# A Perceiver block on one core: half of each pair's 16 turning strips move from SyncE to ScalarE, and the self-attention's divisions run one step later

## The chip, the cores and the metric

The kernel runs on one core of one Trainium2 chip. The time is the device time of one execution in microseconds (us). Three runs of the kernel before took 1126.07, 1129.47 and 1130.55 us; the median is 1129.47 us. Engines are named as the profile names them: PE is TensorE (PEld its weight loads), DVE is VectorE, ACT is ScalarE, POOL is GpSimd, SP is SyncE, which only issues DMAs here. A "q" behind a name (ACTq, SPq) is that engine's sequencer, which issues DMAs and waits on semaphores.

## The reference

Eight batches of 128 rows and 512 columns go through three layers, each added to its input, each after a layernorm without weights:

```python
# cross-attention, 8 heads of 64; context is (8, 2048, 384)
q = (x @ Wq);  k = (context @ Wk);  v = (context @ Wv)
attn = softmax(einsum('bihd,bjhd->bhij', q, k) * 64**-0.5, axis=-1)
x = x + (einsum('bhij,bjhd->bihd', attn, v) @ Wo + bo)
# self-attention over the 128 rows, causal, one head of 512, softmax over the *query* axis
logits = where(causal, -inf, einsum('bik,bjk->bij', queries, keys))
probs = softmax(logits, axis=1) / sqrt(512)
x = x + xn + einsum('bij,bjv->biv', probs, values)     # xn: the normed x
# feed-forward, 2048 hidden units, values rounded to small float formats
x = x + float_quantize(float_quantize(relu(xn @ w1.T + b1)) @ float_quantize(w2).T + bq)
```

All inputs are float32.

## The kernel before, in words

**Steps.** The cross-attention runs as 32 steps: for each batch b (0 to 7) the eight heads are taken as four pairs m (0 to 3), loop at L881 to L950. A step (b, m) does these things:

- `scores` (L549): PE makes eight banks of 128x512 scores (tile `sc`); DVE copies each bank into the SBUF tile `p`, finding the row maxima on the way (L568), and then makes `nm`, the negated and scaled maximum of each head (L576).
- `attend` (L603): PE multiplies the previous pair's turned probabilities `pT` with the values into `po` (L611).
- a **unit**, a generator of PE work that belongs to the next batch or another stage: mostly a k projection or a v projection, written as a product of blocks in 20 small products instead of 24 (`block_product`, L371). Each product is four weight loads and matmuls on the page's rows (two matmuls, each counted with its passes), and takes about 0.86 us of PE. Seven of the results are taken out of PSUM by ACT copies (`take`, L385) and the others are added by DVE (L388, L391).
- `exps` (L579): ACT takes the exponent of each of the two heads in place in `p`, 2.0 us each.
- `turns` (L587): DVE turns `p` in eight pieces as 32x32 squares (L595), four of them after each exponent, and then 16 DMAs, here called **strips**, carry 32 partitions with 4 KB each (128 KB) from `p` to their place in `pT` (L600). Strip (g, a) goes from partitions of group a to partitions of group g; it can start when the two pieces g of the two heads are turned. In 29 of the 32 steps SP issues all 16; in the last three steps, (7, 1) to (7, 3), SP and POOL issue eight each.

There is one `p` tile (apart from one step) and one `pT` tile. So the DVE copies of the next step's scores into `p` wait until the strips have read it, and the strips wait until `attend` has read `pT`.

**Order.** PE, ACT and DVE follow an order written out by hand through the cross-attention (`manual_schedule`, L156, L262, L264): instructions stand on these engines in the order in which the program calls them. The DVE and ACT orders end at L963 and L964; SP's and POOL's orders come from the scheduler. A generator is cut into pieces by `yield`; `first_of` runs it to the next `yield`, `all_of` to its end. In `block_product` the first `yield` (L396) stands after the first of the seven ACT copies, the second (L407) after the fifth. In a usual step ACT's order is: exponent of head 0, copy 1, exponent of head 1, copies 2 to 7. Copy 6 (product 0, output (3, 1)) frees the bank `z2` for product 9, the 13th in PE's order; copy 7 frees `z1` for the 14th.

DMAs that SP and ACT issue share eight completion semaphores, handed out in turn. A DMA waits until the one that had its semaphore before has landed.

**Self-attention.** During the steps (7, 1) to (7, 3) the units are the self-attention of batches 0 to 3: `keys`, `weights_and_values`, `values_and_reads` (L717 to L803). `weights` (L754) makes for each row block r the logits `lg` (L764), their maximum (L768), the exponent `e` on ACT with its sum `den` (L771), and at once the reciprocal (L773) and the scaling (L774) on DVE. `read` (L800) multiplies `e` with the values. The other four batches and the feed-forward follow after the steps.

Of the kernel before, what the change touches and what calls it, by code (L numbers as in the profile page):

```python
# [9 lines left out]
F32 = mybir.dt.float32  # L10
# [7 lines left out]
P = 128  # L18
# [49 lines left out]
def tile_perceiver_block(  # L68
# [21 lines left out]
    nc = tc.nc  # L90
    B, S, D = x.shape
# [18 lines left out]
    SQ = 32  # L110
    Q = P // SQ
# [11 lines left out]
    def bank(name):  # L123
        return ps_one.tile([P, 512], F32, tag="bank", name=name)
# [244 lines left out]
    kts, vts, ps_, sums, qts, turned_, pos, nms, wides = [{} for _ in range(9)]  # L369
# [179 lines left out]
    def scores(b, m):  # L549

        q = qts[b][:, m, :]
        if m == 0:
            sums[b] = small.tile([P, NH], F32, tag="sums", name=f"sums_{b}")
        mx = small.tile([P, 2, NJ], F32, tag="mx", name=f"mx_{b}_{m}", bufs=3)

        home, tag = (ktp, "kt0") if (b, m) == (B - 1, 2) else (pp, "p")
        p = home.tile([P, Q, 2, J // Q], F32, tag=tag, name=f"p_{b}_{m}")
        for n in range(NJ):  # L560
            pair = [bank(f"sc_{b}_{2 * m + i}_{n}") for i in range(2)]
            for i in range(2):
                r = slice(i * DH, (i + 1) * DH)
                nc.tensor.matmul(  # L564
                    pair[i], q[r, :], kts[b, m // 2][r, m % 2, ts(n, 512)], start=True, stop=True
                )
            for i in range(2):
                nc.vector.tensor_scalar(  # L568
                    p[:, :, i].rearrange("p g (t i) -> p t g i", i=SQ)[:, ts(n, Q)],
                    pair[i].rearrange("p (t g i) -> p t g i", g=Q, i=SQ),  # L570
                    1.0, None, ALU.mult, ALU.max, accum_out=mx[:, i, n : n + 1],
                )
        top = small.tile([P, 2], F32, tag="top", name=f"top_{b}_{m}", bufs=3)
        nc.vector.reduce_max(top, mx, axis=AX.X)
        nm = small.tile([P, 2], F32, tag="nm", name=f"nm_{b}_{m}", bufs=3)
        nc.vector.tensor_scalar(nm, top, -SCALE, None, ALU.mult)  # L576
        ps_[b, m], nms[b, m] = p, nm
# [9 lines left out]
    def turns(b, m):  # L587

        p = ps_[b, m]
        pt = ptp.tile([P, Q, 2, J // Q], F32, tag="pT", name=f"pT_{b}_{m}")
        for i in range(2):
            for g in range(Q):
                nc.vector.transpose(p[:, g, i], p[:, g, i])  # L595
        for g in range(Q):
            for a in range(Q):

                eng = nc.gpsimd if b + 1 == B and m > 0 and a % 2 else nc.sync
                eng.dma_start(pt[ts(g, SQ), a], p[ts(a, SQ), g])  # L600
        turned_[b, m] = pt.rearrange("p a h (t i) -> p h t a i", i=SQ)

    def attend(b, m):  # L603


        if m == 0:
            pos[b] = ps_acc.tile([P, NK * S], F32, tag="po", name=f"po_{b}")
        for jt in range(NJT):
            v = vts[b, jt // 8].rearrange("p i t n -> p (i t) n")
            for h in range(2):  # L610
                nc.tensor.matmul(  # L611
                    pos[b][h * DH : (h + 1) * DH, ts(m, P)].rearrange("p (a i) -> p a i", a=Q),
                    v[:, jt % 8, ts(2 * m + h, DH)],
                    turned_[b, m][:, h, jt],
                    start=(jt == 0), stop=(jt == NJT - 1),
                )

    def inverse_sums(b):

        rden = small.tile([P, NH], F32, tag="rden", name=f"rden_{b}")  # L620
        nc.vector.reciprocal(rden, sums[b])
        wide = tmp.tile([P, NH, DH], F32, tag="t", name=f"wide_{b}")
        nc.vector.tensor_copy(wide, rden.unsqueeze(2).to_broadcast([P, NH, DH]))
        wides[b] = wide.rearrange("p h d -> p (h d)")
# [70 lines left out]
    rows = {}  # L695
# [21 lines left out]
    class SelfAttention:  # L717
# [36 lines left out]
        def weights(self, b):  # L754

            i = b % GB
            ps = bank(f"pl_{b}")
            for k in range(NK):
                nc.tensor.matmul(
                    ps[:, :S], self.kt[:, k, ts(i, S)], self.xt[:, k, ts(i, S)],  # L760
                    start=(k == 0), stop=(k == NK - 1),
                )
            lg = self.pool.tile([P, S], F32, tag="lg", name=f"lg_{b}", bufs=2)
            nc.vector.scalar_tensor_tensor(  # L764
                lg, ps[:, :S], c_rows[:, b : b + 1], self.mask, ALU.add, ALU.add
            )
            nm = small.tile([P, 1], F32, tag="snm", name=f"snm_{b}", bufs=4)
            nc.vector.reduce_max(nm, lg, axis=AX.X, negate=True)  # L768
            e = self.pool.tile([P, S], F32, tag="e", name=f"e_{b}", bufs=4)
            den = small.tile([P, 1], F32, tag="sden", name=f"sden_{b}", bufs=4)  # L770
            nc.scalar.activation(e, lg, AF.Exp, bias=nm, accum_out=den)  # L771
            r = small.tile([P, 1], F32, tag="sr", name=f"sr_{b}", bufs=4)
            nc.vector.reciprocal(r, den)  # L773
            nc.vector.tensor_scalar(e, e, r, RSK, ALU.mult, ALU.mult)  # L774
            self.es[b] = e
# [15 lines left out]
            yield  # L791

        def values_and_reads(self, rows):
            for r in rows:
                self.values(r)
            for r in self.rows:
                self.read(r)
            yield
# [7 lines left out]
    def all_of(unit):  # L806
        for _ in unit:
            pass

    def first_of(unit):  # L810
        next(unit)
        return unit
# [68 lines left out]
    for b in range(B):  # L881
        last = b + 1 == B
        for m in range(NK):
            scores(b, m)
            unit = None
            if m > 0:
                attend(b, m - 1)
            elif b > 0:

                attend(b - 1, NK - 1)  # L890
            if m == 0:
                unit = v_proj(b, 1)
            elif not last and m == 1:
                unit = v_proj(b + 1, 0)
            elif not last:
                unit = k_proj(b + 1, m - 2)
            elif m == 1:
                unit = sa0.keys()
            elif m == 2:
                unit = sa0.weights_and_values(sa0.rows[:2])  # L900
            else:
                unit = sa0.values_and_reads(sa0.rows[2:])
            if b == m == 0:

                keys = k_proj(0, 1, (1,))
                first_of(keys)
                first_of(keys)
                exps(b, m, 0)
                all_of(keys)
            else:  # L910
                exps(b, m, 0)
                if unit and not (last and m > 0):
                    first_of(unit)
            exps(b, m, 1)
            if b == m == 0:
                all_of(both_weights())
            if m == 0 and b > 0:
                turned = normalized_first(b - 1)
                if last:
                    bring_last_rows()  # L920
            if m == 1 and b > 0 and not last:
                row_stats(b - 1)
            if m == 2 and b > 0 and not last:
                norm_rows(b - 1)
            turns(b, m)
            if m == 0 and b > 0:
                ot = normalized(b - 1, turned)
            if m == NK - 1:
                inverse_sums(b)
            if unit:  # L930
                all_of(unit)
            if m == 1 and b > 0 and not last:
                row_scale(b - 1)
            if m == 2 and b > 0 and not last:
                nc.scalar.dma_start(xtd[:, :, ts(b - 1, S)], stats[b - 1])
                nc.scalar.dma_start(xr[:, b - 1, :], xs[b - 1])
            if m == 2 and b < B - 2:
                load_x(b)
            if m == 2 and last:
                bring_rows()  # L940
            if m == 3:
                next_half(b + 2, 0)
            if m == 0:
                next_half(b + 1, 1)
                if not last:
                    load_q(b + 1)
                if b > 0:
                    project(b - 1, ot)
                if last:
                    sap, w, sa0 = enter_self_attention()  # L950
    sa1 = SelfAttention(1, sap, w)
# [85 lines left out]
    all_of(sa1.keys())  # L1037
    for r in sa1.rows:
        sa1.weights(r)
    sa1.values(B - 1)  # L1040
    xf0 = normed_rows(0, "xt0")
    for r in sa1.rows:
# [5 lines left out]
    for i in range(1, len(pairs)):  # L1048
        last = i + 1 == len(pairs)
# [66 lines left out]
```

## Time and profile before

| What | Value |
|---|---|
| Runs | 1126.07, 1129.47, 1130.55 us, median 1129.47 |
| The profiled execution's own time | 1125.05 us |
| Its span | 1123.0 us |
| Granted TensorE clock, mean | 0.996 |
| PE busy | 1101.8 us (98% of the span) |
| DVE busy | 812.1 us (72%) |
| ACT busy | 380.8 us (34%) |
| POOL busy | 243.4 us (22%) |
| Strips issued by SP | 488, 128 KB each, median 2.4 us from issue to landing |
| Strips issued by POOL | 24, 128 KB each, median 4.7 us from issue to landing |
| Exponents, 128x2048 | 64, mean 2003 ns |
| Turning pieces on DVE, 128x512 | 256, mean 679 ns |
| ACT copies out of a unit's banks, v and k | 224, mean 589 and 562 ns |

The share of an engine is an average over the stages. DMA-issuing instructions are not counted as busy, so ACT's 34% holds no issue time. In a row of the timeline the first number is the start in us from the span's start, the second the length; the bracket at its end tells the idle time before it and what ended it. In a row of the waits the three numbers are the total in us, how often, and the longest.

### The profile page before, as it was taken

Reading aid. Unit: us, or ns where it says so; the run is one execution under the profiler, and the core shown is the slowest. Engines: PE = TensorE matmul, PEld = TensorE weight load, DVE = VectorE, ACT = ScalarE, POOL = GpSimd, SP = SyncE. Lnnn points to the kernel's source line nnn. Section 1 sums busy time; section 2 is a strip of 40 time slices with the busy share of each in tenths; the row PEclk is TensorE's granted clock in tenths of the full one; section 3 lists DMA queues with packets and bytes.
Section 4 is the critical chain, followed back from the end, with each engine's and each line's share of the span. In section 5 each row is a group of like instructions: output and inputs, shape, how many; then the busy total and the mean of one; then the engine's idle time right before and its main releaser. Section 6 shows DMA issues by size and latency. Waiting matters only on the chain.

```text
span 1123.0 us, 17002 instructions
## 1 busy us (share of the span) xinstructions
PE 1101.8 (98%) x6250; PEld 830.7 (74%) x6254; DVE 812.1 (72%) x1736; ACT 380.8 (34%) x623; POOL 243.4 (22%) x358
## 2 busy tenths in 40 slices
PE   9999999999999999999999999999999979999997
PEld 5485888878777787878787878777887535687775
DVE  5975577778767877878776778767876574976656
ACT  3323333232223232433242232223232321663332
POOL 0244220440044015203500440054001220000001
PEclk9999999999999999999999999999999999999999
DMA  9476235644454455345545644554347475300001
GB/s 328 134 181 169 80 85 120 156 130 112 106 156 115 105 141 133 85 113 150 128 96 122 157 129 114 116 154 108 95 97 223 102 185 192 113 1 20 10 10 38
DMA packets 71858, 134.83 MB, mean 120 GB/s; under 512 B 28240, under 2 KB 36448, under 8 KB 70752
## 3 DMA queue, kind: packets, MB, share of 16 engines
q1 hardware_dynamic: 61120, 113.03, 39.4%
q0 software_dynamic: 3312, 11.03, 3.2%
q10 hardware_dynamic: 7344, 9.70, 2.8%
q8 instruction: 49, 0.80, 0.3%
q14 instruction: 33, 0.27, 0.1%
HBM read 54.01 MB, written 10.49 MB: 57 GB/s over the span
## 4 chain that ended last, share of the span: by engine, by line
PE 91%; DVE 4%; DMA 3%; ACT 1%; SPq 1%; issue 1%; POOL 0%; ACTq 0%; DVEq 0%; POOLq 0%
PE pv_z L488 21%; PE pk_z L465 19%; PE po L611 10%; PE sc L564 10%; PE ph L1012 10%; PE pv_b L488 4%; PE pk_b L465 3%; PE py L690 2%; PE pq L532 2%; PE pf L1024 2%; PE k L447 2%; DMA pT<-p 1%; PE psk L744 1%; PE pw L354 1%; DMA x<-xd 1%; PE psv L780 1%
## 5 line engine op out<-in xcount | busy, mean ns | idle before, releaser
L582 ACT ACTIVATE p<-p,nm 128x2048 f32<-128x2048 f32 x64 | 128.2, 2003 | 437.3 <-DVE nm L576 353.7
L595 DVE STREAM_TRANSPOSE p<-p 128x512 f32<-128x512 f32 x256 | 158.9, 679 | 57.1 <-ACT p L582 56.6
L568 DVE TENSOR_SCALAR_CACHE_REDUCE p<-sc 128x512 f32<-128x512 f32 x256 | 159.0, 686 | 38.0 <-PE sc L564 23.8
L225 POOL TENSOR_TENSOR m<-x 128x256 f32<-128x256 f32 x70 | 51.2, 732 | 504.3 <-DMA x<-in_ctx_t_dram 409.6
L488 PE MATMUL pv_z<-wv_sums,x 128*128 128x256 f32 x640 | 157.9, 381 | 0.0
L465 PE MATMUL pk_z<-x,wk_sums 128*128 128x256 f32 x600 | 149.9, 382 | 1.0 <-ACT kt L385 0.6
L611 PEld LDWEIGHTS po<-pT,v 128*64 128x64 f32 x2048 | 112.9, 138 | 31.0 <-issue 29.5
L488 PEld LDWEIGHTS pv_z<-wv_sums,x 128*128 128x128 f32 x640 | 120.5, 190 | 18.6 <-issue 2.2
L564 PE MATMUL sc<-kt,q 64*128 64x512 f32 x512 | 127.7, 605 | 1.8 <-DVE p L568 1.8
L465 PEld LDWEIGHTS pk_z<-x,wk_sums 128*128 128x128 f32 x600 | 112.4, 190 | 20.7 <-DVE kt L391 1.3
L611 PE MATMUL po<-pT,v 128*64 128x128 f32 x2048 | 120.6, 276 | 6.6 <-DMA pT<-p 6.6
L1012 PE MATMUL ph<-xf,w 128*128 128x256 f32 x512 | 111.3, 379 | 0.0
L1012 PEld LDWEIGHTS ph<-xf,w 128*128 128x128 f32 x512 | 97.2, 190 | 13.9 <-issue 0.5
L488 PE MATMUL pv_z<-wv_sums,m 128*128 128x256 f32 x448 | 107.3, 379 | 0.0
L465 PE MATMUL pk_z<-m,wk_sums 128*128 128x256 f32 x420 | 101.4, 379 | 0.0
L564 PEld LDWEIGHTS sc<-kt,q 64*128 64x128 f32 x512 | 50.4, 186 | 67.1 <-issue 52.8
L488 PEld LDWEIGHTS pv_z<-wv_sums,m 128*128 128x128 f32 x448 | 83.4, 190 | 12.6 <-issue 0.5
L465 PEld LDWEIGHTS pk_z<-m,wk_sums 128*128 128x128 f32 x420 | 78.4, 190 | 11.8 <-DVE kt L388 0.4
L385 ACT COPY v<-pv_z 128x512 f32<-128x512 f32 x112 | 62.9, 589 | 55.6 <-PE pv_z L488 55.4
L385 ACT COPY kt<-pk_z 128x512 f32<-128x512 f32 (+1 forms) x112 | 59.8, 562 | 51.2 <-PE pk_z L465 50.6
L225 POOL TENSOR_TENSOR x<-x 128x256 f32<-128x256 f32 x98 | 70.1, 734 | 0.4 <-DMA x<-in_ctx_t_dram 0.4
L388 DVE TENSOR_TENSOR v<-pv_z,v 128x512 f32<-128x512 f32 x96 | 63.1, 684 | 5.5 <-PE pv_z L488 5.5
(200 smaller groups left out, 1254.7 us busy)
## 6 DMA issues: line engine op xcount, KB each, us to landing
pT<-p SPq DMA_DIRECT2D x488, 128.0 KB, 2.4
x<-in_ctx_t_dram SPq DMA_DIRECT2D x45, 512.0 KB, 5.6
w<-in_w_t_dram SPq DMA_DIRECT2D x1, 4096.0 KB, 12.4
w2f<-in_w_t_dram SPq DMA_DIRECT2D x16, 256.0 KB, 2.8
pT<-p POOLq DMA_DIRECT2D x24, 128.0 KB, 4.7
x_in<-in_x_dram SPq DMA_DIRECT2D x8, 256.0 KB, 6.8
qd<-xq SPq DMA_DIRECT2D x8, 256.0 KB, 2.5
q<-qd SPq DMA_DIRECT2D x8, 256.0 KB, 3.3
```

The costliest lines, as they stand in the source:

```text
L225: eng.tensor_tensor(x_block(b, h, to), x_block(b, h, one), x_block(b, h, two), ALU.add if op == "+" else ALU.subtract,)
L385: nc.scalar.copy(outs[ij], views(ps))
L388: nc.vector.tensor_tensor(outs[to], views(ps), outs[other], op)
L447: nc.tensor.matmul(pss[j], wk4[:, k, f2, j, :], xraw[0, 0][:, k, 2 * n : 2 * n + 2], start=(k == 0), stop=(k == NKC - 1),)
L465: nc.tensor.matmul(ps[:, ts(i, BK)], wk_sums[:, WSLOT[WAT[r]], f2, :], x_block(b, h, XAT[r]), start=start and i == 0, stop=True, skip_grou ...
L488: nc.tensor.matmul(ps[:, ts(t, 256)], x[:, ts(t, P)], wv_sums[:, WSLOT[WAT[r]], :], start=start and t == 0, stop=True, skip_group_check=True,)
L564: nc.tensor.matmul(pair[i], q[r, :], kts[b, m // 2][r, m % 2, ts(n, 512)], start=True, stop=True)
L568: nc.vector.tensor_scalar(p[:, :, i].rearrange("p g (t i) -> p t g i", i=SQ)[:, ts(n, Q)], pair[i].rearrange("p (t g i) -> p t g i", g=Q, ...
L582: nc.scalar.activation(p[:, :, i], p[:, :, i], AF.Exp, bias=nms[b, m][:, i : i + 1], scale=SCALE, accum_out=sums[b][:, h : h + 1],)
L595: nc.vector.transpose(p[:, g, i], p[:, g, i])
L611: nc.tensor.matmul(pos[b][h * DH : (h + 1) * DH, ts(m, P)].rearrange("p (a i) -> p a i", a=Q), v[:, jt % 8, ts(2 * m + h, DH)], turned_[b, ...
L1012: nc.tensor.matmul(ps[:, :n], w1[:, k, ts(c, P)], xt[:, k, at], start=(k == 0), stop=(k == NK - 1),)
```

## The change

Of the 16 strips of a step, SP issues the eight with g of 0 and 1. The eight with g of 2 and 3 are issued by ACT, after the unit has been run to its next `yield`, that is, after copy 5 and ahead of copies 6 and 7. This holds for 29 steps; in (7, 1) to (7, 3) SP and POOL share the strips as before. In step (0, 0), whose unit has not been started by then, ACT's strips stand after copy 1.

The reciprocal and the scaling of the self-attention's probabilities move out of `weights` into a function of their own, `probabilities`. For batches 0 to 3 it is called in the next step, (7, 3), and for batches 4 to 7 after all four `weights`. The tile `lg` has four buffers instead of two.

```diff
@@ turns(b, m)
-        for g in range(Q):
-            for a in range(Q):
-                eng = nc.gpsimd if b + 1 == B and m > 0 and a % 2 else nc.sync
-                eng.dma_start(pt[ts(g, SQ), a], p[ts(a, SQ), g])
         turned_[b, m] = pt.rearrange("p a h (t i) -> p h t a i", i=SQ)
+        def strips(eng, gs, rows=range(Q)):
+            for g in gs:
+                for a in rows:
+                    eng.dma_start(pt[ts(g, SQ), a], p[ts(a, SQ), g])
+        return strips
@@ SelfAttention.weights(b)
-            lg = self.pool.tile([P, S], F32, tag="lg", name=f"lg_{b}", bufs=2)
+            lg = self.pool.tile([P, S], F32, tag="lg", name=f"lg_{b}", bufs=4)
...
             nc.scalar.activation(e, lg, AF.Exp, bias=nm, accum_out=den)
+            self.es[b] = e, den
+
+        def probabilities(self, b):
+            e, den = self.es[b]
             r = small.tile([P, 1], F32, tag="sr", name=f"sr_{b}", bufs=4)
             nc.vector.reciprocal(r, den)
             nc.vector.tensor_scalar(e, e, r, RSK, ALU.mult, ALU.mult)
@@ SelfAttention.values_and_reads(rows)
+            for r in self.rows:
+                self.probabilities(r)
             for r in rows:
                 self.values(r)
@@ the loop over the steps
-            turns(b, m)
+            strips = turns(b, m)
+            if last and m > 0:
+                strips(nc.sync, range(Q), range(0, Q, 2))
+                strips(nc.gpsimd, range(Q), range(1, Q, 2))
+            else:
+                strips(nc.sync, range(Q // 2))
             if m == 0 and b > 0:
                 ot = normalized(b - 1, turned)
             if m == NK - 1:
                 inverse_sums(b)
+            if not (last and m > 0):
+                first_of(unit)
+                strips(nc.scalar, range(Q // 2, Q))
             if unit:
                 all_of(unit)
@@ after the steps
     for r in sa1.rows:
         sa1.weights(r)
+    for r in sa1.rows:
+        sa1.probabilities(r)
```

## The prediction

> **What bounds the kernel.** I read the page's busy times and chain first, then the waits of PE, then the timeline of one usual step, (0, 2).
>
> ```profile
> PE 1101.8 (98%) x6250; PEld 830.7 (74%) x6254; DVE 812.1 (72%) x1736; ACT 380.8 (34%) x623; POOL 243.4 (22%) x358
> PE 91%; DVE 4%; DMA 3%; ACT 1%; SPq 1%; issue 1%; POOL 0%; ACTq 0%; DVEq 0%; POOLq 0%
> ...
> PE po L611 <- DMA pT<-p: 6.6, 2, 6.0
> PE sc L564 <- DVE p L568: 1.8, 2, 1.5
> ```
>
> PE is the bound from end to end. Its waits for strips sum to 6.6 us, of which 6.0 are one wait in step (7, 3), whose strips stay where they are. So a faster path for the strips has little to win; what it does to PE's other suppliers decides. The step:
>
> ```profile
> 165.22 2.49 DVE L595 STREAM_TRANSPOSE p<-p 128x512 f32<-128x512 f32 x4 [0.68 <-ACT p L582]
> ...
> 166.00 10.83 SPq L600 DMA_DIRECT2D pT<-p  x16
> ...
> 166.92 0.59 ACT L385 COPY kt<-pk_z 128x512 f32<-128x512 f32 x1 [0.28 <-PE pk_z L465]
> ...
> 169.51 0.58 ACT L385 COPY kt<-pk_z 128x512 f32<-128x512 f32 x1 [2.00 <-PE pk_z L465]
> ...
> 170.38 0.58 ACT L385 COPY kt<-pk_z 128x512 f32<-128x512 f32 x1 [0.28 <-PE pk_z L465]
> ...
> 171.04 1.03 PE L465 MATMUL pk_z<-x,wk_sums 128*128 128x256 f32 x4
> ```
>
> The three ACT rows are copies 5, 6 and 7. Copy 6 waits for product 0 (2.00 us idle) and ends at 170.09; the PE row is product 9, which adds into the bank that copy 6 empties. Copy 6 takes 0.58 us and about 0.1 us goes to the hand-over, so it may start at 170.4 at the latest. The change puts eight DMA issues between copies 5 and 6.
>
> **Part 1, the issues on ACT.** A sequencer passes nothing while it issues: POOL's memset starts when the issue ahead of it ends, and ACT's three issues of a later step follow one another.
>
> ```profile
> 860.06 0.56 POOL L709 DMA_DIRECT2D u<-line  x1
> 860.60 0.24 POOL L831 MEMSET mask<- 128x128 f32 x1
> ...
> 274.36 0.59 ACTq L935 DMA_DIRECT2D xtd<-xt_s  x1
> 274.99 0.66 ACTq L936 DMA_DIRECT2D xr<-x  x1
> 275.68 0.78 ACTq L648 DMA_DIRECT2D x<-xd  x1
> ```
>
> No row shows ACT computing right behind an issue; that it waits as POOL does is the assumption everything rests on. ACT's first strip needs the seventh turning piece. SP's first, at 166.00, needs the fifth; two more at 0.60 us give 167.2, and copy 5 has been started by then. From 167.2 to 170.4 there are 3.2 us, or 0.40 us an issue.
>
> An issue of a strip on ACT is not in the trace. Bounds: ACT's cheapest issue, of 128 rows of 2 KB, takes 0.33 us (0.36 with the gap), so 2.9 us for eight and copy 6 at 170.1: no stall. SP alone issues strips at 0.63 us (16 in 10.03 us below): 5.0 us, copy 6 at 172.2, stall 1.8 us. Where SP shares with POOL, in (7, 1), SP's eight take 7.18 us: copy 6 at 174.4, stall 4.0 us. At 1.2 us each, the longest there, it would be 9.6 us and a stall of 6.4 us.
>
> ```profile
> 215.48 10.03 SPq L600 DMA_DIRECT2D pT<-p  x16
> ...
> 872.71 7.18 SPq L600 DMA_DIRECT2D pT<-p  x8
> ...
> L600 SPq DMA_DIRECT2D pT<-p x8: 507/786/1227, 872.7 to 878.7; - x8
> ...
> 169.00:172.00 3.00, 3.00 (x16) 2.64 (x15) 0.76 (x2) 1.17 (x2) 0.00 (x0) 1.00 0.98 205
> ...
> 918.00:922.00 4.00, 1.91 (x5) 0.57 (x3) 3.09 (x7) 0.29 (x1) 0.24 (x1) 1.00 1.05 254
> ```
>
> The last two rows say why sharing is slow: one queue's strips already hold the DMA engines at a share of 0.98 with 205 GB/s, and two queues reach 254. ACT's issues will be held back as SP's are in (7, 1). But there both queues start within 0.5 us; here SP has two strips out when ACT starts, and is done first. I take the middle of 5.0 and 7.2, 6.1 us: copy 6 at 173.3, a stall of 2.9 us. The shared semaphores agree: the 16th strip waits for the eighth to land, which at 0.52 to 0.64 us a strip (128 KB at 254 and 205 GB/s) and a first landing at 168.3 is 171.9 to 172.8, so the last issue ends at 172.5 to 173.4.
>
> Behind the issues wait, on ACT, copies 6 and 7; behind copy 6, DVE's addition into the same output and PE's products 13 to 20 with the next step's scores. DVE's additions (0.69 us) are shorter than a product (0.86 us), so they follow PE and add nothing. There are 32 units with seven copies; three end before step (0, 0) and one is its own. In the other 28 copies 5 and 6 start 2.59 us apart, as here: 28 x 2.9 = **+81.2 us**.
>
> In step (0, 0) ACT's strips stand after copy 1 (113.10), when DMA is free: 5.0 us, copy 2 at 118.1, done at 118.8; the seventh product needs it at 111.34 + 6 x 0.863 = 116.5: **+2.3** (0 to 4.5).
>
> The issues of L935, L936 and L648 behind copy 7 start some 3 us later; the next user is the next step's strips or later: 0. SP's loads of context and q come up the queue sooner but wait for PE then (27.0, 7.5 and 24.2 us of SP's waits name PE): 0. POOL's order is unchanged: 0.
>
> **Part 2, strips that land sooner.** In some steps DVE may not write `p` yet and PE's scores stretch over their 3.63 us:
>
> ```profile
> 361.33 4.00 PE sc L564 x16
> 365.32 3.64 PE po L611 x64
> ...
> 386.88 4.69 PE sc L564 x16
> ```
>
> In the chain seven such pieces sum to 4.4 us over 3.63 each. The steps that end at 286.84, 496.26 and 603.02 take 1.1, 1.4 and 2.7 us more than their like. With PE later by 2.9 us and the strips no later, all goes: **-9.6** (0 to -9.6).
>
> **Part 3, the divisions.** In (7, 2) DVE waits four times 0.56 us for an exponent and divides between; the last score copies start only at 903.18. Without that, PE's banks allow them at 900.8: the exponents, turns and strips of (7, 3) and `po` at 925.90 come 2.4 us sooner. The divisions (4 x 0.45 us) then stand ahead of two additions that PE's reads need, and the reads may slide by 1.8 us; PE is idle from 919.9 to 925.9 anyway, and still has 3.6 us. **-2.4** (0 to -2.4). For batches 4 to 7 PE has the values and transposes ahead of the reads and no wait there: 0.
>
> **Sum.** 81.2 + 2.3 - 9.6 - 2.4 = +71.5 on the profiled 1125.05 gives 1196.6. The median of the runs lies 4.4 above the profiled execution; forecast for the median: **1201 us**.
>
> [...]
>
> **Rivals** (times for the median, parts 2 and 3 as above).
> - *Cheap issues, faster.* If ACT's issue stays at 0.36 us, copy 6 is in time and -12.0 remains: 1117. For it: ACT's rows of 0.33. Against: SP takes 0.33 us for 2 KB rows too, and 0.5 to 0.6 for these strips. It decides below 0.40 us an issue. Chance 0.10.
> - *No measurable change.* Stalls of 0.15 to 0.55 us a step cancel the gains; a narrow gap between the other cases. 0.04.
> - *Issues at SP's undisturbed pace.* Stall 1.8 us: 50.4 + 2.3 - 12.0 = +40.7, 1170. For it: in-step rows of SP; against: the DMA share. 0.22.
> - *The forecast*, stalls of 2.2 to 3.6 us, 1181 to 1221. 0.42.
> - *ACT held as long as SP in (7, 1).* Stall 4.0 us: +102, 1232. 0.16.
> - *Every issue at 1.2 us.* Stall 6.4 us: +169.5, 1299. 0.06.
>
> A change under 0.5% (5.6 us) can't be told from none. Faster 0.10, same 0.04, slower the rest, 0.86. The range leaves out the first two and the last, 0.2: from a little under 1170 to a little over 1232.
>
> **What will show it.** In the profile after, ACTq has rows L601 of eight issues with 5 to 7 us in all; copy 6 starts 5.7 to 7.1 us after copy 5 instead of 2.59; PE's waits name ACT's copies in 28 steps with about 2.9 us; scores no longer stretch. If PE's waits don't name ACT, or ACT's copies start beside its issues, part 1 is wrong. If the eight issues take under 3 us, the first rival holds. In (7, 3) PE's wait for `pT` should fall from 6.0 to about 3.6 us.

## The result and the profile after

The changed kernel takes 1245.09 us (median of four executions, 1239.23 to 1245.74), against 1127.77 us for the kernel before (1124.27 to 1130.55): a ratio of 1.1031, 95% interval 1.0990 to 1.1072. The forecast was 1201 us, with a range from a little under 1170 to a little over 1232 us. The direction held; the time is 44 us above the point and 13 us above the 1232 us of the last case that the range takes in. The profiled execution took 1239.23 us, its span 1237.5 us.

Where the time went is read from the starts of `po` (the values' product of each step), which divide the span into the forecast's parts:

| Stretch | Before, us | After, us | Change | Forecast |
|---|---|---|---|---|
| start to the first `po`, step (0, 0) | 132.17 | 134.78 | +2.6 | +2.3 |
| that `po` to that of step (7, 0): the 28 steps | 732.28 | 842.16 | +109.9 | +71.6 (81.2 less 9.6) |
| to the `po` of step (7, 3) | 61.45 | 65.10 | +3.65 | -2.4 |
| the rest | 197.1 | 195.5 | -1.6 | 0 |

The -1.6 us of the rest was not followed up; the executions of the kernel before differ by more (1124.27 to 1130.55 us).

First the page of the kernel after: the busy times (busy us, share of the span, instructions) and the shares of the chain that ended last.

```profile
PE 1128.4 (91%) x6254; PEld 844.7 (68%) x6254; DVE 824.6 (67%) x1736; ACT 378.4 (31%) x623; POOL 243.3 (20%) x358
...
PE 77%; DMA 12%; ACTq 3%; DVE 3%; ACT 2%; issue 1%; SPq 1%; DVEq 0%
```

PE was 98% busy and is now 91% busy. But the idle time alone does not account for the loss: the busy time has also grown, from 1101.8 to 1128.4 us, with the same matmuls. In the chain, strips and ACT's sequencer have taken the place of PE. The waits of PE and of ACT in the kernel after (total us, times, longest):

```profile
PE pv_z L488 <- ACT v L385: 44.4, 15, 3.8
PE pk_z L465 <- ACT kt L385: 44.1, 15, 3.9
PE po L613 <- DMA pT<-p: 9.0, 2, 7.5
```

```profile
ACT v L385 <- DMA pT<-p: 88.7, 15, 6.9
ACT kt L385 <- DMA pT<-p: 86.3, 14, 6.9
```

PE waits 88.5 us for copies on ACT; before, such waits were 0.6 us. ACT's copies in turn stand behind the strips, six us each time. The page names the landing of a strip as the releaser, since ACT's last issues wait for shared semaphores (1.3 us of a step, in the mean, ends with the landing of the DMA that had the semaphore before); most of the hold is the issuing itself (4.96 us of issue time in 6.45 us from the first issue to the end of the last, mean of the 28 steps). The next view is the timeline of the step that the forecast worked on, (0, 2), in the kernel after (start, length, engine, line, tiles; in brackets the idle time before and what ended it):

```profile
173.44 6.69 SPq L601 DMA_DIRECT2D pT<-p  x8
...
174.36 0.59 ACT L385 COPY kt<-pk_z 128x512 f32<-128x512 f32 x1 [0.28 <-PE pk_z L465]
174.64 6.41 ACTq L601 DMA_DIRECT2D pT<-p  x8
...
181.09 0.58 ACT L385 COPY kt<-pk_z 128x512 f32<-128x512 f32 x1 [6.14 <-DMA pT<-p]
...
181.73 1.18 PE L465 MATMUL pk_z<-x,wk_sums 128*128 128x256 f32 x4 [3.09 <-ACT kt L385]
...
182.70 3.57 PE L465 MATMUL pk_z<-m,wk_sums 128*128 128x256 f32 x8
...
186.11 1.89 PE L465 MATMUL pk_z<-x,wk_sums 128*128 128x256 f32 x8
```

Copy 5 starts at 174.36, ACT issues its eight strips from 174.64 on, and copy 6 starts at 181.09, 6.7 us after copy 5 instead of 2.59. PE waits 3.09 us. Then comes what the forecast did not have: the next eight matmuls take 3.57 us, and the eight after them 1.89 us, for equal work. The same step by stretches of time (start and end, length, busy time of PE, PEld, DVE, ACT and POOL with their instructions, granted clock of TensorE, share of the DMA engines, GB/s):

```profile
174.00:178.30 4.30, 4.30 (x22) 3.75 (x20) 2.32 (x4) 0.67 (x2) 0.00 (x0) 1.00 0.86 214
178.30:181.70 3.40, 0.34 (x2) 0.00 (x0) 0.69 (x1) 0.61 (x2) 0.00 (x0) 1.00 1.01 277
...
182.70:186.10 3.40, 3.40 (x9) 2.70 (x8) 2.08 (x3) 0.00 (x0) 0.00 (x0) 0.50 0.30 84
186.10:190.50 4.40, 4.40 (x21) 3.61 (x19) 3.45 (x5) 0.00 (x0) 0.00 (x0) 1.00 0.01 2
```

Behind 3.4 us with hardly any matmul, from 182.7 on, 1 us after the wait's end, the granted clock is 0.50 for 3.4 us, and PE does 9 matmuls where some 16 fit at the pace of the next row (21 in 4.40 us). A busy PE in such a row is a slow PE, not one with more to do: that is why its busy time grew.

### The profile page after: what moved, and what is told of

The parts are those of the page before. It is cut to its first block, busy times and chain, and to the rows that moved or that the text cites. A ratio compares the mean times of both kernels' runs of the same rounds, so it can differ in the third digit from the quotient of the medians.

```text
span 1237.5 us, 17018 instructions
## 1 busy us (share of the span) xinstructions
PE 1128.4 (91%) x6254; PEld 844.7 (68%) x6254; DVE 824.6 (67%) x1736; ACT 378.4 (31%) x623; POOL 243.3 (20%) x358
## 4 chain that ended last, share of the span: by engine, by line
PE 77%; DMA 12%; ACTq 3%; DVE 3%; ACT 2%; issue 1%; SPq 1%; DVEq 0%
PE pv_z L488 18%; PE pk_z L465 16%; DMA pT<-p 12%; PE po L613 10%; PE sc L564 9%; PE ph L1029 9%; ACTq L601 3%; PE py L692 2%; PE pq L532 2%; PE pf L1041 2%; PE k L447 2%; PE pv_b L488 1%; ACT v L385 1%; PE psk L746 1%; PE pw L354 1%; ACT kt L385 1%
## 5 line engine op out<-in xcount | busy, mean ns | idle before, releaser
L488 PE MATMUL pv_z<-wv_sums,x 128*128 128x256 f32 x640 | 163.4, 391 | 41.9 <-ACT v L385 41.9
L465 PE MATMUL pk_z<-x,wk_sums 128*128 128x256 f32 x600 | 153.9, 390 | 44.4 <-ACT kt L385 44.1
L488 PE MATMUL pv_z<-wv_sums,m 128*128 128x256 f32 x448 | 120.2, 414 | 2.5 <-ACT v L385 2.5
L564 PE MATMUL sc<-kt,q 64*128 64x512 f32 x512 | 118.5, 602 | 0.0
L465 PE MATMUL pk_z<-m,wk_sums 128*128 128x256 f32 x420 | 109.3, 402 | 0.0
L488 PEld LDWEIGHTS pv_z<-wv_sums,m 128*128 128x128 f32 x448 | 91.8, 209 | 18.9 <-ACT v L385 2.9
L388 DVE TENSOR_TENSOR v<-pv_z,v 128x512 f32<-128x512 f32 x96 | 66.0, 691 | 56.6 <-ACT v L385 30.7
L388 DVE TENSOR_TENSOR kt<-pk_z,kt 128x512 f32<-128x512 f32 (+1 forms) x96 | 62.9, 657 | 55.7 <-ACT kt L385 33.0
L465 PEld LDWEIGHTS pk_z<-m,wk_sums 128*128 128x128 f32 x420 | 83.9, 203 | 14.0 <-DVE kt L388 0.4
L564 PEld LDWEIGHTS sc<-kt,q 64*128 64x128 f32 x512 | 46.8, 186 | 59.7 <-issue 55.4
```

The lines of the kernel that those rows point to most:

```text
L388: nc.vector.tensor_tensor(outs[to], views(ps), outs[other], op)
L465: nc.tensor.matmul(ps[:, ts(i, BK)], wk_sums[:, WSLOT[WAT[r]], f2, :], x_block(b, h, XAT[r]), start=start and i == 0, stop=True, skip_grou ...
L488: nc.tensor.matmul(ps[:, ts(t, 256)], x[:, ts(t, P)], wv_sums[:, WSLOT[WAT[r]], :], start=start and t == 0, stop=True, skip_group_check=True,)
L564: nc.tensor.matmul(pair[i], q[r, :], kts[b, m // 2][r, m % 2, ts(n, 512)], start=True, stop=True)
```

## The experiments

The expectations name the theories by letters. **A**: ACT's issues hold copies 6 and 7 longer than the room that PE leaves them, and what is lost with the divisions comes from a load that now starts sooner. **B**: the divisions save what the forecast said. **C**: two queues hamper each other, so that ACT's strips cost much wherever they stand. **D**: the loss goes with the number of strips that ACT issues between the copies, and there is no room that is free. **E**: the half clock comes from PE's idling. **F**: it does not, and busy matmuls in the wait would change nothing. The code cuts are against the changed kernel, unless the text says otherwise.

### The strips alone

The divisions' part of the change is taken back; the strips stay where the change puts them.

```diff
-            self.es[b] = e, den
-        def probabilities(self, b):
-            e, den = self.es[b]
             r = small.tile([P, 1], F32, tag="sr", name=f"sr_{b}", bufs=4)
             nc.vector.reciprocal(r, den)
...
         def values_and_reads(self, rows):
-            for r in self.rows:
-                self.probabilities(r)
```

> Only the strips are split between SP and ACT; the divisions of the self-attention stand where they stood before. Theory A (the loss is the strips' issues between ACT's copies 5 and 6; the divisions made it about 4 us worse, because ACT reaches the 1.5 MB load of the rows sooner and it meets the strips of step (7, 2)): about 1241 us, PE's wait for pT in (7, 2) back near 1 us, in (7, 3) near 6 us. Theory B (the divisions gained their 2.4 us as forecast): about 1247 us.

Measured: 1240.03 us (1235.49 to 1246.09), ratio 1.1018 (1.0979 to 1.1057). Its waits:

```profile
PE pv_z L488 <- ACT v L385: 44.9, 15, 3.8
PE pk_z L465 <- ACT kt L385: 42.9, 15, 4.0
PE po L613 <- DMA pT<-p: 6.7, 2, 5.9
```

The strips carry the loss: the same waits for ACT, 87.8 us, and nearly the same time. The stretch from the `po` of (7, 0) to that of (7, 3) is 61.47 us here, as before (61.45), so the 3.65 us lost there belong to the divisions.

The four executions of this kernel differ more than usual, and with the clock: spans of 1233.7, 1237.8, 1238.7 and 1244.3 us have mean granted clocks of 0.975, 0.972, 0.972 and 0.968.

### ACT's strips after copies 6 and 7

```diff
-            if not (last and m > 0):
-
-                first_of(unit)
-                strips(nc.scalar, range(Q // 2, Q))
             if unit:
                 all_of(unit)
+            if not (last and m > 0):
+                strips(nc.scalar, range(Q // 2, Q))
```

The divisions stay as before. All sixteen strips are still issued by SP and ACT, eight each.

> Strips split as in the first kernel of this group, but ACT issues its eight after copies 6 and 7 of the unit instead of between copies 5 and 6. Theory A (copies queued behind the issues make PE wait, and nothing else): PE's waits for ACT's copies vanish, the granted clock goes back to 0.99 or more, and the time is 1120 to 1130 us. Theory C (two hardware queues at once are slow by themselves, through the DMA engines or the semaphores that they share): strips land late, PE waits for pT or DVE for p, and the time stays above 1150 us.

Measured: 1115.05 us (1113.73 to 1117.22), ratio 0.9905 (0.9887 to 0.9924). The step (0, 2) in its timeline:

```profile
166.05 4.95 SPq L601 DMA_DIRECT2D pT<-p  x8
...
169.57 0.59 ACT L385 COPY kt<-pk_z 128x512 f32<-128x512 f32 x1 [2.00 <-PE pk_z L465]
...
170.43 0.59 ACT L385 COPY kt<-pk_z 128x512 f32<-128x512 f32 x1 [0.28 <-PE pk_z L465]
170.44 5.12 ACTq L601 DMA_DIRECT2D pT<-p  x8
171.09 1.03 PE L465 MATMUL pk_z<-x,wk_sums 128*128 128x256 f32 x4
```

Copies 6 and 7 come when product 0 is done, and PE goes on without a wait. Theory C expected over 1150 us and falls: the issues cost ACT 5.12 us here too, but nothing is behind them that PE needs. The stretch of the 28 steps is 722.75 us against 732.28 before. These 9.5 us are what strips that land sooner are worth; the forecast said 9.6. They are the stretched scores: from the first start to the last, the scores of the 28 steps exceed their shortest length by 9.6 us in sum before, and by nothing here.

### Four strips between the copies

ACT keeps only the strips of group 2 (four) between copies 5 and 6, SP issues twelve; the divisions as before.

```diff
-                strips(nc.sync, range(Q // 2))
+                strips(nc.sync, (0, 1, 3))
...
-                strips(nc.scalar, range(Q // 2, Q))
+                strips(nc.scalar, (2,))
```

> ACT issues only the four strips with g = 2 at the same place between copies 5 and 6; SP issues the other twelve. Theory A (there are 3.2 us of room; only what goes beyond stalls PE): four issues take about 2.5 us, so PE waits under 0.3 us a step, no half-clock stretches, 1115 to 1130 us, perhaps some us under before since fewer scores wait for strips. Theory D (every issue on ACT costs its time): half of the loss, about 1185 us.

Measured: 1119.39 us (1117.88 to 1119.82), ratio 0.9939 (0.9922 to 0.9955). PE's waits:

```profile
PE po L613 <- DMA pT<-p: 5.1, 2, 3.5
...
PE pk_z L465 <- ACT kt L385: 0.8, 2, 0.6
```

ACT is held 2.59 us by four issues (mean of the steps), less than the 3.2 us that the forecast read as the room before copy 6. The waits for its copies are as small as before (0.8 us, against 0.6), although a quarter of the strips still stands between the copies: the loss is not in proportion to the issues, and D falls.

### Six strips between the copies

```diff
                 strips(nc.sync, range(Q // 2))
+                strips(nc.sync, (3,), (2, 3))
...
-                strips(nc.scalar, range(Q // 2, Q))
+                strips(nc.scalar, (2,))
+                strips(nc.scalar, (3,), (0, 1))
```

ACT issues six between copies 5 and 6, SP ten; the divisions as before. A wait of half the length asks whether the loss of clock comes with every wait or only with long ones.

> ACT issues six strips between copies 5 and 6 (g = 2 all four, g = 3 the first two), SP ten, divisions as before. Theory A (stall = hold beyond 3.2 us): copy 6 starts about 4.9 us after copy 5, PE waits some 1.3 us a step, 36 us in all, less some 9 us from strips that land sooner. Theory E (the clock halves only after idle near a whole stretch of 3.4 us): no half-clock stretches in these steps, so about 1155 us. If the clock fell with every idle, 16 or more stretches would show and the time would be about 1180 us.

Measured: 1162.86 us (1162.35 to 1163.92), ratio 1.0317 (1.0289 to 1.0345).

```profile
PE pv_z L488 <- ACT v L385: 20.1, 15, 2.5
PE pk_z L465 <- ACT kt L385: 18.7, 15, 2.3
```

ACT is held 4.72 us, and PE waits 38.8 us in 30 waits. The mean clock is 0.994: from the start of one matmul to the next these waits are mostly 1.5 to 1.9 us, and only one in the steps (2.64 us) was followed by a half clock; the longest (2.84 us) was not. With 2.59, 4.72 and 6.45 us of hold for four, six and eight issues, the room of 3.2 us is the point of decision: 4.72 less 3.2 is 1.5 us a step, where the waits' mean is 1.3 us. By the waits the room was a little larger, 3.4 us, with six issues as with eight.

### PE kept busy in the wait

Into the first kernel above (strips alone), six matmuls of 128x128 by 128x256 are put on PE just ahead of the product that waits. They write to a bank that a later product overwrites, so the output is the whole computation.

```diff
         mm(b10, 10, True)
+        if filling:
+            for _ in range(6):
+                nc.tensor.matmul(b16[:, :BK], wv_sums[:, 0, :P],
+                                 wv_sums[:, 1], start=True, stop=True)
```

`filling` is set in step (0, 1), so that it works in the 28 steps. The profile counts each of the six with its two passes, as x12.

> As the first kernel of this group, with six extra matmuls of 128x128 by 128x256 whose result is overwritten, put on PE just ahead of the place where it waits for copy 6, in the 28 steps after (0, 0). They take about 2.6 us of the wait of about 3.1 us. Theory E (idle of some 3 us brings the clock to half for 3.4 us in 16 of the 28 steps, 1.7 us each): the copies come at the same time, PE stays busy, the clock stays at 0.99 or more, and the time falls by about 27 us, to about 1214 us. Theory F (the matmuls after the wait are slow for another reason, such as DMA traffic): the clock stays near 0.97 and the time stays at about 1241 us.

Measured: 1215.42 us (1212.43 to 1215.84), ratio 1.0788 (1.0764 to 1.0811). The step (0, 2) in its timeline:

```profile
179.16 2.75 PE L420 MATMUL pk_b<-wv_sums 128*128 128x256 f32 x12
...
181.71 0.59 ACT L387 COPY kt<-pk_z 128x512 f32<-128x512 f32 x1 [6.07 <-DMA pT<-p]
...
182.34 1.13 PE L470 MATMUL pk_z<-x,wk_sums 128*128 128x256 f32 x4 [0.43 <-ACT kt L387]
...
183.31 1.89 PE L470 MATMUL pk_z<-m,wk_sums 128*128 128x256 f32 x8
```

and its span and mean granted clock,

```profile
core 0: 1214.0 us, clock 0.995
```

against those of the kernel without the added matmuls:

```profile
core 0: 1237.8 us, clock 0.972
```

Copy 6 is as late as before (6.07 us of idle on ACT) and its product starts no sooner, but the eight matmuls behind it take 1.89 us, not 3.57, and the kernel with more work on PE is 24.6 us faster. E expected 1214 us, F 1241 us. So it is PE's idling that brings the half clock here. One wait of the filled kernel was still followed by a half clock: that of step (0, 0), 2.90 us long, which is not filled.

### The divisions alone

This is the kernel before with only the divisions moved (`probabilities`, the four `lg` buffers and the two places that call it, as in the change).

> Only the divisions of the self-attention move; all strips stay with SP as before. Theory A (ACT reaches the 1.5 MB load of the rows some 3 us sooner, and it shares the DMA engines with the last strips of step (7, 2)): PE's wait for pT in (7, 2) is 5 to 8 us instead of 0.7, the wait in (7, 3) shrinks by some 2 to 4 us, and the time is 0 to 4 us over the kernel before. Theory B (the divisions gain as forecast): 2.4 us under the kernel before, waits of 0.7 to 2 and about 3.6 us.

Measured: 1127.80 us (1126.36 to 1131.22), ratio 1.0014 (0.9999 to 1.0028). The interval touches no change, but the place is clear: from the `po` of (7, 0) to that of (7, 3) it takes 64.14 us against 61.45. In step (7, 2) of the kernel before, ACT issues the load of `rows` (1.5 MB) here, and `po` starts here:

```profile
901.06 0.33 ACTq L704 DMA_DIRECT2D rows<-xr  x1
```

```profile
905.70 3.71 PE L611 MATMUL po<-pT,v 128*64 128x128 f32 x64 [0.66 <-DMA pT<-p]
```

With the divisions alone moved, ACT's issue and the two `po`:

```profile
899.90 0.33 ACTq L704 DMA_DIRECT2D rows<-xr  x1
```

```profile
911.91 6.59 PE L611 MATMUL po<-pT,v 128*64 128x128 f32 x64 [6.29 <-DMA pT<-p]
...
930.56 3.71 PE L611 MATMUL po<-pT,v 128*64 128x128 f32 x64 [1.56 <-DMA pT<-p]
```

The first strip of (7, 2) is issued at 893.88 before and at 895.85 here. So the load stood 7.2 us behind it, when all 16 strips had been issued, and now stands 4.05 us behind it, when 13 had been. The strips take 15.7 us from the first issue to the last landing instead of 11.4, and PE waits 6.29 us instead of 0.66. The `po` behind the long wait also runs at half clock at first (6.59 us instead of 3.71). The wait of (7, 3) fell from 5.99 to 1.56 us.

### The divisions, with the load of rows a step earlier

```diff
-            if m == 2 and last:
+            if m == 1 and last:
                 bring_rows()
```

added to the kernel of the last section: ACT issues the load at the end of step (7, 1), ahead of the strips.

> As the first kernel of this group, and the 1.5 MB load of the rows is issued by ACT at the end of step (7, 1) instead of (7, 2), when the strips of (7, 1) have mostly landed. Theory A: without the collision the divisions' gain shows: strips of (7, 2) land within 11.5 us of their first issue, PE's waits for pT are about 2 us in (7, 2) and 3.6 us in (7, 3), and the time is 2 to 3 us under the kernel before. If the rows' load is not the cause, (7, 2) still waits 5 to 8 us.

Measured: 1125.44 us (1119.74 to 1129.05), ratio 0.9979 (0.9963 to 0.9995).

```profile
884.40 0.33 ACTq L704 DMA_DIRECT2D rows<-xr  x1
```

```profile
908.11 3.71 PE L611 MATMUL po<-pT,v 128*64 128x128 f32 x64 [2.20 <-DMA pT<-p]
...
926.04 5.38 PE L611 MATMUL po<-pT,v 128*64 128x128 f32 x64 [3.72 <-DMA pT<-p]
```

The wait of (7, 2) is down to 2.20 us. That of (7, 3) is 3.72 us, the forecast's "about 3.6". The stretch is 59.32 us, 2.1 us shorter than before and 4.8 us shorter than with the load in its old place. The 2.20 us are no loss: the scores ahead of that `po`, which were stretched before, no longer are, and it starts 20.18 us after the one before it, against 20.04. So in this stretch the divisions' move does save what the forecast said, once the load is out of the way; and it was the load that took it. The totals are too close to show it: the medians differ by 1.0 us, and the 28 steps, which this change leaves as they are, by 2.4 us between the two profiles. The load was not moved by itself. It has little to gain there: with the load behind them (kernel before) the strips of (7, 2) land within 11.4 us, without it within 11.5.

### Both moves in their better places

The changed kernel with ACT's strips after copies 6 and 7 and the load of `rows` a step earlier.

> ACT's eight strips after copies 6 and 7, the divisions a step later, and the rows' load at the end of (7, 1). If the parts add up: 1115 us (strips after the copies) less 2 to 3 us, 1112 us, with every step from (0, 1) to (7, 0) at its shortest length of before and PE's waits for pT under 5 us together.

Measured: 1112.76 us (1111.82 to 1114.42), ratio 0.9871 (0.9848 to 0.9895): faster than the kernel before by 13.7 us, and than the changed kernel by 132 us.

```profile
PE 1093.6 (98%) x6254; PEld 827.3 (75%) x6254; DVE 812.0 (73%) x1736; ACT 381.4 (34%) x623; POOL 243.2 (22%) x358
...
PE po L613 <- DMA pT<-p: 4.5, 2, 2.5
```

PE is again 98% busy, with 8 us less of it: stretched scores are gone from its busy time. The 28 steps take 722.73 us and the last stretch 59.60 us. Against the kernel with the strips alone moved (ratio 0.9905) the intervals touch, so the total does not prove that the divisions add to it; the last stretch, 61.60 us there, does agree.

## Why the prediction was right or wrong

**Part 1, the issues on ACT: right, and nearly to size.** The assumption "everything rests on", that ACT passes nothing on while it issues, held: copy 6 starts 0.04 us after the end of the last issue in each of the 28 steps. (What stands ahead of an issue does run beside it: copy 5 of the step (0, 2) from 174.36 to 174.95, the issues from 174.64 on.) The eight issues hold ACT for 6.45 us in the mean of the steps (5.99 to 7.42), where the forecast took 6.1 as the middle of its two bounds. Of that, 4.96 us are the issues, some 0.6 us each, and 1.5 us gaps between them, 1.3 us of these waits for shared semaphores. Copies 5 and 6 are 6.67 us apart (forecast 5.7 to 7.1). PE's waits in the 28 steps sum to 88.5 less 2.5 in (0, 0) and 0.6 ahead of it, 85.4 us, 3.05 each: the forecast's 2.9 and 81.2 were 4 us short. The part up to step (0, 0) took 2.6 us more, against 2.3. That this fits so closely is in part luck: with the strips alone moved it took 5.3 us more, since there the same wait was followed by a half clock.

**The sum: it had no term for the clock, and that is the step that failed.** It took a stall to cost its own length and no more. In 16 of the 28 steps the granted clock falls to 0.50 for 3.413 us behind the wait, in which PE does half the work (9 matmuls in the stretch from 240.71 below, 18 in that from 394.30, at 1.00): 16 times 1.7 us are 27.3 us. The filled kernel shows it from the other side, 24.6 us faster with the same late copies. Added up for the 28 steps: 85.4 of waits, 27.3 of half clock and 28 times 0.15 us for the first four matmuls behind a wait (1.18 us instead of 1.03), less 9.5 for part 2, is 107.4, against 109.9 measured. The whole changed kernel takes some 5 us longer in the median than in the profiled execution. The clock accounts for most of it: the other executions' mean clocks are 0.968 to 0.970, where this one has 0.972, which is some 4 us by estimate (the span times what the clock lacks to 1: 34.7 us here, 37.3 to 39.8 us there).

Which waits are followed by a half clock can be read from the trace. All 18 stretches at half clock of the profiled execution start on one grid of 3.413 us: divided by 3.4133 us, their starts leave the same remainder, 1.78 us. What counts is how much of a wait falls into one field of the grid. Here are the fields of two waits in the kernel after, of 3.03 us from one matmul to the next (up to 239.54) and of 3.56 us (up to 392.42):

```profile
237.30:240.71 3.41, 1.17 (x5) 1.06 (x6) 1.00 (x2) 1.07 (x2) 0.00 (x0) 1.00 1.02 244
240.71:244.12 3.41, 3.41 (x9) 2.70 (x8) 2.25 (x4) 0.00 (x0) 0.00 (x0) 0.50 0.01 1
387.48:390.89 3.41, 1.76 (x9) 1.20 (x7) 0.69 (x1) 0.00 (x0) 0.00 (x0) 1.00 0.99 280
390.89:394.30 3.41, 1.88 (x9) 1.71 (x10) 1.36 (x2) 2.58 (x4) 0.00 (x0) 1.00 0.98 228
394.30:397.71 3.41, 3.41 (x18) 3.00 (x17) 3.27 (x6) 1.55 (x3) 0.00 (x0) 1.00 0.12 29
```

The shorter wait leaves PE idle for 2.24 us of one field (3.41 less 1.17), and the next field runs at 0.50. The longer one is split, 1.65 us in one field and 1.53 in the next, and the clock stays at 1.00. So with all 28: the 16 waits with 1.97 us or more in one field were followed by a half clock, the 12 with 1.93 us or less were not. With the strips alone moved, 15 waits with 2.00 us or more were and 13 with less were not; with six strips, one (2.15 us) was and 27 (up to 1.88 us) were not. How many of the waits are halved thus hangs on where the grid happens to lie.

The stretches are 3.413 us long, but idling near a whole stretch, as theory E has it for the six strips, is not needed: some 2.0 us in one field were enough. The 28 gaps from one matmul to the next are 3.03 to 4.26 us here, and 16 of them were followed by a half clock; with six strips they are mostly 1.5 to 1.9 us, and one was.

**Part 2, strips that land sooner: right.** In the profile after, the scores of the 28 steps take 3.63 us each, and with the copies left alone the 28 steps gain 9.5 us (forecast 9.6).

**Part 3, the divisions: wrong in sign.** The forecast's "the exponents, turns and strips of (7, 3) and `po` at 925.90 come 2.4 us sooner" left out one instruction that moves with the exponents. ACT's order has the load of `rows` next to the last exponent of the self-attention. Divisions no longer between the exponents bring ACT there three us sooner, in the middle of the strips of (7, 2). In the changed kernel:

```profile
1010.40 0.33 ACTq L706 DMA_DIRECT2D rows<-xr  x1
```

```profile
1023.61 6.42 PE L613 MATMUL po<-pT,v 128*64 128x128 f32 x64 [7.48 <-DMA pT<-p]
...
1042.03 3.71 PE L613 MATMUL po<-pT,v 128*64 128x128 f32 x64 [1.51 <-DMA pT<-p]
```

The sign to look for, the wait of (7, 3), fell even lower than announced, to 1.51 us, and the saving was lost one step earlier, in a wait of 7.48 us, with a `po` partly at half clock behind it (6.42 us instead of 3.71), that the forecast did not look at.

**The rivals.** Issues at ACT's cheapest pace fall: 0.6 us each, not 0.36. Issues at SP's undisturbed pace (a stall of 1.8 us) fall narrowly: the issuing itself took the 5.0 us that this rival named, but the gaps between the issues add 1.5. A hold as long as SP's in (7, 1), stall 4.0 us, named 1232 us and comes nearest in time, for a reason that did not occur. And the forecast's own case, stalls of 2.2 to 3.6 us, holds with 3.05 us; only its time, 1181 to 1221 us, was wrong, by the missing term.

**Strips from two issuers.** The 16 strips took 10.55 us from the first issue to the last landing in the mean of the steps after, against 11.8 us for SP's undisturbed ones before. ACT's eight issues held it for 6.45 us, 4.96 us of it issue time, beside SP's eight with 4.96 us.

**The load once more.** With ACT's strips after the copies and the divisions as before, the load comes no sooner, 7.2 us behind the first strip, and yet the strips of (7, 2) take 14.2 us instead of 11.4. Here are the last three strips that SP issues and the load, in the kernel before:

```profile
898.01 3.34 SPq L600 DMA_DIRECT2D pT<-p  x3
901.06 0.33 ACTq L704 DMA_DIRECT2D rows<-xr  x1
```

and with ACT's strips after the copies:

```profile
888.61 3.38 SPq L601 DMA_DIRECT2D pT<-p  x3
891.59 0.33 ACTq L706 DMA_DIRECT2D rows<-xr  x1
```

Before, the last strip's issue ends at 901.35, ahead of the load's at 901.39; here it ends at 891.99, behind the load's at 891.92, and only this last strip lands late. The same holds in the other kernels that have the divisions as before: where the load's issue ends first (four strips, six strips) the strips take 14.2 and 14.9 us, where it ends last (strips alone, filled) 11.5 us. So the kernel before escaped this collision by less than 0.05 us, and the forecast did not see how near it was. The total hardly notices it: (7, 2) loses 2.9 us and (7, 3) gains 2.7.

**Open.** The line of 2.0 us was read from waits for ACT's copies alone; with the divisions moved in the kernel before, with and without the early load, one stretch at half clock in the 28 steps follows stretched scores with only 1.2 to 1.4 us of waiting in the field before. The busy times of matmuls are modelled, so the line is not exact.

## What to carry to other kernels

DMAs issued on ACT took their time out of its own order here (eight strips: 4.96 us of issues, 6.45 us from the first to the end of the last). So where a computing engine is to issue, read the room before the next instruction that the bound engine needs, and place only as many issues as fit (here 3.2 to 3.4 us: four of 0.6 us fitted, six did not), or put them behind it. When a stall of some 3 us recurs on PE, look at the granted clock behind it as well as at the waits: here it added a third to the stalls' price. Shorter stalls (1.5 to 1.9 us with six strips: one half clock in 28 steps) and filled ones (24.6 us faster) were spared most of that price. And when work is taken out of an engine's path, follow every instruction that now comes sooner, loads above all, to what it collides with.

## What the runs showed of the hardware that was not expected

- A granted clock of 0.50 for 3.413 us behind 16 of 28 waits of PE, each 3.0 to 4.3 us from one matmul to the next, seen in the timeline as 3.57 us for eight matmuls that take 1.89 us otherwise. The stretches lie on a fixed grid; some 2.0 us of idling in one field of it bring one, and a longer wait that is split between two fields can pass.
- SP and ACT issue beside each other at 0.62 us a strip each in the mean, hardly slower than SP alone (0.60 us), and the two queues together moved 277 GB/s in a stretch of 3.4 us, where SP's strips alone moved 205 in one of 3 us.
- A single load of 1.5 MB, issued 3 us sooner, stretched 16 strips from 11.4 to 15.7 us; and where its issue ended some 0.1 us ahead of the last strip's, that strip landed 3 us late.
